# A two-layer graph network on one Trainium2 core: the first level of a top-p search from one ScalarE pass instead of two

## The chip, the cores and the metric

The kernel runs on one core of a Trainium2 chip. The core has TensorE (PE in the profile; PEld is its weight load), VectorE (DVE), ScalarE (ACT), GpSimd (POOL) and SyncE (SP, which issues DMAs). Each engine works through its own instructions in their order and waits at semaphores for the others.

The metric is the device time of one execution in microseconds. Before the change three executions took 1310.96, 1312.36 and 1307.9 us, with a median of 1310.96 us. The profile comes from a further execution that took 1361.88 us, of which the span from the first instruction to the last is 1360.1 us.

## The reference, cut to what matters

There are N = 2708 nodes with 256 features. Layer 0 multiplies a sparse adjacency matrix with the features. Layer 1 takes two steps; in each, every row of a softmax over all nodes is cut to its largest entries, which together hold 0.9 of the mass ("top-p"), and the cut rows multiply the features.

```python
def _top_p_attention(X, W1, W2, W3):
    q = X @ W1.T @ W2.T
    k = X @ W3.T
    logits = q @ k.T / TAU
    probs = jax.nn.softmax(logits, axis=-1)
    idx = jnp.argsort(-probs, axis=-1)
    sp = jnp.take_along_axis(probs, idx, axis=-1)
    cs = jnp.cumsum(sp, axis=-1)
    keep_sorted = cs - sp < TOP_P
    ...
    return A / jnp.maximum(A.sum(-1, keepdims=True), 1e-12)

for n in range(STEPS):
    A = _top_p_attention(Xa, W1, W2, W3)
    Xf = R @ Xf
    Xa = A @ Xa
    Z = Z + Xf @ U1[n].T + Xa @ U2[n].T
```

R is the row-normalised input to layer 1 (the adjacency with ones added on the diagonal). Two layer norms follow.

## The kernel before

The 2708 rows are cut into 22 blocks of 128 rows (the last, the "edge" block, has 20). A block's row of exponentials, 128 x 2708 numbers in float32, lies in SBUF as a tile `e`. In step 2 a row keeps too many entries for them to be sorted, so the cut is searched. Two trial levels `l0` and `l1` are tried; from what lies above each, the next is computed. A last level `l2` or `l1` is chosen; DVE then takes the largest 48 of what lies just below it and finds the cut among them exactly.

**Trying a level.** `try_act` (line 961) does it on ACT for blocks 1 to 21, `try_dve` (line 989) on DVE for block 0. With z the sum of a row's exponentials, an entry lies above the level when l*e > z. On ACT a try has two passes over the 2708 entries. Part 0 (line 966) is a Relu of l*e - z with its sum in `relu`; part 1 (line 969) is a Sign of the same with its sum in `sign`. Part 2 (line 972) turns the sum of signs into the count `n` of entries above the level; part 3 (line 974) makes `u` = relu/z + n, which is l times the mass above the level, and calls `next_level` (line 977): a line in l and u with the fitted constants `STEPS` (lines 979 and 980), and after the second try also `few` (line 982). On DVE one instruction (line 993) sums the entries above the level.

**The pipeline of step 2.** The loop at line 1272 runs 24 periods `per`, each of six slots `g`. In period `per` four blocks are under way at once:

- block per + 2 gets its logits from PE and its exponentials from ACT (`exps2`, lines 844 to 848, in slots 0, 1 and 3);
- block per + 1 has its levels tried on ACT;
- block per goes through `last_level` (lines 1003 to 1013), `below_level` (line 1023) and `candidates` (line 1030) on DVE; block per - 1 goes through `in_order`, `threshold`, `mark` (line 1083) and `mask` (line 1088) there;
- block per - 2 is turned on PE (`turn`, line 527), copied from PSUM to SBUF by ACT as `wT` (line 530) and multiplied on PE (`products`, line 564).

Beside these, PE works off the sparse product R with Xf in units of one 128 x 128 piece (`r_units`, line 749), three or so in a slot. Their right-hand sides `yg` are gathered by POOL's indirect DMAs (line 719). From period 12 on, rows that are done go through the layer norms, of which two to four 128 x 256 passes in slot 0 are ACT's (line 1192).

**What sets the order.** Nothing is scheduled automatically: the order of the calls in the loop is the order in each engine's queue. In one slot the calls are: turn, logits, r_units, products of the slot before, exps2, the parts of `try_act` for this slot, then DVE's share. In period `per` DVE first needs the end of the try of slot 3 of the period before: `last_level` reads `few`, `l1`, `u1`, `l2` and `relu`. In slot 5 of each period DVE runs `begin_search` (lines 852 to 857) of block per + 2, which needs the sum of the third exponential.

**Buffers that matter here.** `wT` and the PSUM tile `tr` have two buffers each, the PSUM tile `lg` of the logits has one, and `yg` has two.

**When the search fails.** Every row sets flags, such as one for more than 48 entries between level and cut. If any flag is set, the program runs `general_path`, which computes layer 1 again in a slow way. It is not run in the profile.

Of the kernel before, what the change touches and what calls it, by code (L numbers as in the profile page):

```python
# [11 lines left out]
AF = mybir.ActivationFunctionType  # L12
ALU = mybir.AluOpType
# [4 lines left out]
TOP_P = 0.9  # L18
# [12 lines left out]


GUESS = 2.76141059
STEPS = ((0.93339875, 14.44678062, 82.55022771), (0.98700001, 8.00991560, 128.06811957))
FEW = 20.0
TOP_S = 0.8999
TIE_EPS = 1.5e-5
KS = 7
# [110 lines left out]
def fast_path(ctx, tc, c, flags, fint, xT_d, x_d, w0_d, b0_d, w1_d, w2_d, w3_d, u1_d, u2_d, g_d, b_d):  # L149
    nc = tc.nc  # L150
    N, D, DA, NB, DC, KH, CHS, rows = c.N, c.D, c.DA, c.NB, c.DC, c.KH, c.CHS, c.rows
# [17 lines left out]
    def ps_acc(t=None):  # L169
        acc = ps.tile([P, CH], FP, tag="acc", name="acc")  # L170
        if t == NB - 1:
            nc.vector.memset(acc[:, :D + 1], 0.0)
        return acc
# [426 lines left out]
    def exps1(t):  # L600

        p = rows(t)
        e = es[t % 4]
        nmax, srt = st1[t]
        z = small.tile([P, 2], FP, tag="z1", name="z1", bufs=3)
        st1[t] = (srt, z)
        h = 11 * P

        def part(i):
            if i == 0:  # L610
                nc.scalar.activation(srt[:p], srt[:p], AF.Exp, bias=nmax[:p], scale=1.0)
            a, b = ((0, h), (h, N))[i]
            nc.scalar.activation(e[:p, a:b], e[:p, a:b], AF.Exp, bias=nmax[:p], scale=1.0,
                                 accum_out=z[:p, i:i + 1])
        return part
# [147 lines left out]
    def za_load(m):  # L763


        if loads.get(m):
            loads[m] = 2
            return None
        loads[m] = 1
        base = work.tile([P, D], FP, tag="in", name="base", bufs=3)  # L770
        nc.sync.dma_start(out=base[:rows(m)], in_=za_d[m * P:m * P + rows(m), :])
        return base
# [35 lines left out]
    def e2(t):  # L808
        return ring[t % 5]
# [30 lines left out]
    def shift(b, lg):  # L840
        nc.vector.tensor_reduce(b.nmax, lg[:, :P], AX.X, ALU.max, negate=True)
# [8 lines left out]
    def begin_search(b):  # L850

        nc.vector.tensor_reduce(b.z, b.all[:b.p, :NL], AX.X, ALU.add)
        yield
        nc.vector.reciprocal(b.rz, b.z)
        nc.vector.tensor_scalar(b.nz, b.z, -1.0, None, op0=ALU.mult)
        yield
        nc.vector.tensor_scalar(b.l0, b.roots, b.roots, b.rz, op0=ALU.mult, op1=ALU.mult)
# [21 lines left out]
    part = exps1(0)  # L879
# [5 lines left out]
    part = exps1(1)  # L885
# [11 lines left out]
    for t in range(NB):  # L897
        acc = ps_acc(t)
        part = exps1(t + 2) if t + 2 < NB else None
        b = None  # L900
        if t >= NB - 3:
            b = blocks[t - (NB - 3)] = Block(t - (NB - 3))
# [52 lines left out]
    w = tile1[:, NW:]  # L955
# [5 lines left out]
    def try_act(b, k, part):  # L961


        e = e2(b.t)[:b.p, :N]
        if part == 0:
            nc.scalar.activation(scr[:b.p, :N], e, AF.Relu, bias=b.nz, scale=b.l[k], accum_out=b.relu)  # L966
            return
        if part == 1:
            nc.scalar.activation(scr[:b.p, :N], e, AF.Sign, bias=b.nz, scale=b.l[k], accum_out=b.sign)  # L969
            return  # L970
        if part == 2:
            nc.scalar.activation(b.n, b.sign, AF.Identity, bias=halfn[:b.p], scale=0.5)
            return
        nc.scalar.activation(b.u[k], b.relu, AF.Identity, bias=b.n, scale=b.rz)
        next_level(b, k)

    def next_level(b, k):
        keep, slope, down = STEPS[k]
        nc.scalar.activation(b.kept, b.l[k], AF.Copy, scale=keep + TOP_P * slope, bias=-down)
        nc.scalar.activation((b.l1, b.l2)[k], b.u[k], AF.Identity, bias=b.kept, scale=-slope)  # L980
        if k:
            nc.scalar.activation(b.few, b.l1, AF.Copy, scale=TOP_P, bias=-FEW)

    def level(b, l):

        nc.vector.reciprocal(b.d, l)
        nc.vector.tensor_scalar(b.d, b.d, b.z, None, op0=ALU.mult)

    def try_dve(b, k):

        e = e2(b.t)[:b.p, :N]
        level(b, b.l[k])
        nc.vector.scalar_tensor_tensor(w[:b.p, :N], e, b.d, e, op0=ALU.is_ge, op1=ALU.mult, accum_out=b.m)
        nc.vector.tensor_scalar(b.u[k], b.m, b.rz, b.l[k], op0=ALU.mult, op1=ALU.mult)
        if k == 0:
            keep, slope, down = STEPS[0]
            nc.vector.tensor_scalar(b.kept, b.l0, keep + TOP_P * slope, -down, op0=ALU.mult, op1=ALU.add)
            nc.vector.scalar_tensor_tensor(b.l1, b.u0, -slope, b.kept, op0=ALU.mult, op1=ALU.add)

    def last_level(b):  # L1000
# [109 lines left out]
    def vector_slots(a, b, begin):  # L1110


        if b and b.t == 0:
            run_all(in_order(b))
            yield
            run_all(threshold(b))
            yield
            for i in range(WS):
                mark(b, i)
            yield  # L1120
            mask(b)
            yield
            run_all(last_level(a))
            below_level(a)
            yield
            run_all(candidates(a))
            run_all(begin)
            yield
            return
        order = in_order(b) if b else None  # L1130
        levels = last_level(a) if a else None
        cands = candidates(a) if a else None
        limits = threshold(b) if b else None
        run_all(turns((part_of_it(order, 7) if b else None, 1), (levels, 1)))
        yield
        if a:
            below_level(a)
        yield
        run_all(turns((order, 1), (part_of_it(cands, 8) if a else None, 2)))
        if a and not b:  # L1140
            run_all(part_of_it(cands, 8))
        yield
        run_all(turns((limits, 1), (cands, 2)))
        yield
        if b:
            mark(b, 0)
            mark(b, 1)
        yield
        for i in (2, 3):
            if b:  # L1150
                mark(b, i)
            if begin:
                next(begin)
        if begin:
            run_all(begin)
        if b:
            mask(b)
        yield
# [113 lines left out]
    for per in range(NB + 2):  # L1272
        if per == NB + 1:
            tail.append(True)
        n_r = units.get(per, 0)
        b_act = blocks.get(per + 1)
        t_mul = per - 2 if per > 1 else None
        if t_mul is not None:
            accs[t_mul] = ps_acc(t_mul)
        b_exp = None  # L1280
        if per and per + 2 < NB:
            b_exp = blocks[per + 2] = Block(per + 2)
        vector = vector_slots(blocks.get(per), blocks.get(per - 1), begin_search(b_exp) if b_exp else None)
        for g in range(NG):
            n = n_r * (g + 1) // NG - n_r * g // NG
            now = later.pop(0)
            later.append([])
            if g == 0:
                if b_exp:
                    shift(b_exp, lg[0])  # L1290
                r_units(n)
            if t_mul == EDGE:
                if g == 0:
                    products(0)
                    edge_product(ya, accs[EDGE], e2(EDGE))
            elif t_mul is not None:
                turn(t_mul, g, ya, accs[t_mul], e2(t_mul))
            if b_exp and g == 3:
                lg = logits(1, b_exp.t, 2)
            if g == NG - 1 and 3 < per + 3 < NB:  # L1300
                lg = logits(1, per + 3, 0)
            if g:
                r_units(n)
            if b_exp and g == 1:
                lg = logits(1, b_exp.t, 1)
            if t_mul is not None and t_mul != EDGE:
                products(1)
            if b_exp and g in (0, 1, 3):
                exps2(b_exp, (g + 1) // 2, *lg)
            if b_act:  # L1310
                for k, part in {0: ((0, 0),), 1: ((0, 1), (0, 2), (0, 3)), 2: ((1, 0),), 3: ((1, 1), (1, 2), (1, 3))}.get(g, ()):
                    try_act(b_act, k, part)
            next(vector)
            if g == 0:
                final_slot(0)
                if t_mul:
                    t = t_mul - 1
                    base = za_load(t)
                    later[0].append(lambda t=t, base=base: arrive(t, base, accs.pop(t), ras.pop(t)[:rows(t)]))
            for f in now:  # L1320
                f()
            if g and (per < NB + 1 or g < NG - 1):
                final_slot(g)
# [4 lines left out]
    for f in later[0] + later[1]:  # L1328
# [10 lines left out]
                                   op0=ALU.mult, op1=ALU.is_lt)  # L1339
# [391 lines left out]
```

## Time and profile before

| what | us |
|---|---|
| three executions, median | 1310.96 |
| profiled execution | 1361.88 |
| its span | 1360.1 |
| of the span: pipeline of step 2, first `below_level` to the last | 779.0 to 1300.6 |
| ACT: 43 Relu passes (line 966), all of step 2 | 113.6 |
| ACT: 42 Sign passes (line 969), all of step 2 | 110.9 |
| ACT idle in the 25.20 us period from 1126.36 | 2.90 |
| DVE idle in that period | 1.61 |
| PE idle in that period | 1.41 |

The table's idle times are a period's length less the busy time of the engine in it. A period is counted here from one `below_level` instruction on DVE to the next, which is a little after the start of slot 1. The groups of the page give the busy sum of a line and the mean duration of one instruction. The table of windows gives, for each stretch, every engine's busy time and the number of instructions. "Idle before" tells what an engine waited for; "issue" in that place means that no wait which the profile shows ended there. PE's ends are modelled, so its busy time holds some hidden waiting.

### The profile page before, as it was taken

To read this page: it belongs to the slowest core of one execution; us is meant where nothing else is said; L and a number is where in the kernel's file an instruction comes from. 1 tells how busy PE (TensorE), PEld (TensorE's weight loads), DVE (VectorE), ACT (ScalarE), POOL (GpSimd) and SP (SyncE) were. 2 spreads that over 40 slices of the span, in tenths; PEclk is the share of its full clock that TensorE was granted. 3 is DMA by queue.
4 is the path that set the end of the run, shared out by engine and by line. 5 is a ranking of instruction groups with operands and counts; after the bars stand their busy time and mean duration, and the time that the engine had idled before them with its cause. 6 is when DMAs were issued, how large, how long until landed. Compare 5 with 4: busy or idle time off the path is not lost.

```text
span 1360.1 us, 18883 instructions
## 1 busy us (share of the span) xinstructions
PE 1250.1 (92%) x5764; PEld 895.5 (66%) x5764; DVE 998.1 (73%) x3406; ACT 733.8 (54%) x1337; POOL 635.2 (47%) x594
## 2 busy tenths in 40 slices
PE   8999999988999999999997959999996999999985
PEld 6877877733567777666774727766664776666763
DVE  2544545866888888877840469878877899999995
ACT  1011011035455565555553577877786898998931
POOL 1000000014554533777563177777743668888850
PEclk9999999989899999999998969999998999999997
DMA  6554545513222110232222245645543444554541
GB/s 186 163 176 155 166 155 160 165 54 117 81 92 67 55 57 10 89 94 95 69 73 74 68 150 157 188 140 175 172 111 109 148 159 143 171 181 151 169 111 33
DMA packets 101993, 166.27 MB, mean 122 GB/s; under 512 B 17394, under 2 KB 74358, under 8 KB 101882
## 3 DMA queue, kind: packets, MB, share of 16 engines
q1 hardware_dynamic: 75596, 108.91, 24.7%
q0 software_dynamic: 20544, 51.17, 13.6%
q10 hardware_dynamic: 5742, 4.89, 1.3%
q8 instruction: 48, 0.79, 0.2%
q14 instruction: 63, 0.52, 0.1%
HBM read 130.87 MB, written 34.03 MB: 121 GB/s over the span
## 4 chain that ended last, share of the span: by engine, by line
PE 67%; ACT 19%; DVE 6%; issue 4%; another core or an unknown queue 2%; DMA 0%; ACTq 0%; DVEq 0%
PE acc L564 22%; PE acc L257 15%; PE lg L507 8%; PE tr L527 5%; PE misc L749 5%; ACT e L969 4%; ACT e L966 3%; ACT e L844 3%; ACT wT L530 3%; PE acc L651 2%; PE acc L462 2%; PE misc L426 2%; PE misc L392 2%; PE acc L672 2%
## 5 line engine op out<-in xcount | busy, mean ns | idle before, releaser
L530 ACT COPY wT<-tr 128x512 f32<-128x512 f32 (+2 forms) x258 | 131.7, 518 | 254.7 <-PE tr L527 153.3
L564 PE MATMUL acc<-ya,wT 128*128 128x256 f32 (+1 forms) x924 | 234.6, 394 | 18.8 <-ACT wT L530 12.1
L564 PE MATMUL acc<-x,wT 128*128 128x256 f32 (+1 forms) x924 | 234.6, 393 | 13.2 <-ACT wT L530 12.9
L719 POOL DMA_INDIRECT yg<-v_d,ix x154 | 190.1, 1234 | 79.4 <-issue 32.3
L564 PEld LDWEIGHTS acc<-x,wT 128*128 128x128 f32 (+1 forms) x924 | 167.2, 192 | 87.8 <-issue 40.6
L719 POOL DMA_INDIRECT yg<-yf_d,ix x154 | 192.6, 1250 | 62.3 <-issue 36.2
L564 PEld LDWEIGHTS acc<-ya,wT 128*128 128x128 f32 (+1 forms) x924 | 169.8, 193 | 75.6 <-issue 28.1
L257 PE MATMUL acc<-y,adj_t 128*128 128x257 f32 (+1 forms) x924 | 208.4, 381 | 0.0
L367 POOL DMA_INDIRECT adj_t<-in_adj,ix x154 | 170.3, 1106 | 51.4 <-issue 42.4
L749 PE MATMUL misc<-yg,adj_t 128*128 128x256 f32 (+1 forms) x704 | 183.5, 395 | 11.4 <-issue 6.6
L257 PEld LDWEIGHTS acc<-y,adj_t 128*128 128x128 f32 (+1 forms) x924 | 171.8, 189 | 32.7 <-issue 8.9
L507 PE MATMUL lg<-k,q 64*128 64x512 f32 (+3 forms) x528 | 151.9, 602 | 29.7 <-issue 11.2
L749 PEld LDWEIGHTS misc<-yg,adj_t 128*128 128x128 f32 (+1 forms) x704 | 125.7, 191 | 61.7 <-issue 31.2
L527 PE MATMUL tr<-ident,e 128*128 128x128 f32 (+2 forms) x946 | 147.0, 274 | 2.3 <-DVE e L1088 2.3
L527 PEld LDWEIGHTS tr<-ident,e 128*128 128x128 f32 (+2 forms) x946 | 113.6, 139 | 41.5 <-issue 17.6
L334 POOL DMA_DIRECT2D part_d<-e x1 | 0.6, 576 | 286.2 <-DVE e L333 286.2
L966 ACT ACTIVATE e<-e,st 128x2708 f32<-128x2708 f32 (+1 forms) x43 | 113.6, 2641 | 0.1
L570 DVE MAX8 cand<-e 128x8 f32<-128x170 f32 (+1 forms) x352 | 87.6, 318 | 32.7 <-ACT e L514 15.4
L969 ACT ACTIVATE e<-e,st 128x2708 f32<-128x2708 f32 (+1 forms) x42 | 110.9, 2641 | 0.1
L439 ACT COPY x1T<-tr 128x256 f32<-128x256 f32 (+1 forms) x22 | 8.0, 364 | 186.6 <-PE tr L438 186.6
L1030 DVE MAX8 cand<-w 128x8 f32<-128x136 f32 (+1 forms) x440 | 106.2, 285 | 0.0
L507 PEld LDWEIGHTS lg<-k,q 64*128 64x128 f32 (+1 forms) x528 | 39.3, 183 | 64.2 <-issue 35.6
(237 smaller groups left out, 1762.9 us busy)
## 6 DMA issues: line engine op xcount, KB each, us to landing
adj_t<-in_adj SPq DMA_DIRECT2D x44, 704.0 KB
adj_t<-adjc_d SPq DMA_DIRECT2D x44, 448.0 KB
adjc_d<-adj_t SPq DMA_DIRECT2D x22, 256.0 KB
base<-za_d SPq DMA_DIRECT2D x41, 128.0 KB
adjc_d<-adj_t SPq DMA_DIRECT2D x22, 192.0 KB
xt<-in_x ACTq DMA_DIRECT2D x21, 128.0 KB
x_d<-x SPq DMA_DIRECT2D x21, 128.0 KB
x1b_d<-xb SPq DMA_DIRECT2D x21, 128.0 KB
```

Of the source, the lines that this page charges most:

```text
L257: nc.tensor.matmul(acc[:p, :n], lhsT=halves[k // KH][:kw, k % KH, :p], rhs=y[:kw, k, :n], start=k == 0, stop=stop and k == NB - 1)
L367: nc.gpsimd.indirect_dma_start(out=a[:CW, i, :], out_offset=None, in_=adj_rows, in_offset=bass.IndirectOffsetOnAxis(ap=ix[:CW, m, i:i + 1] ...
L507: nc.tensor.matmul(lg[:p, h, :b - a], lhsT=q[o, t * P:t * P + p], rhs=keys[s][o, i, :b - a], start=True, stop=True)
L527: nc.tensor.transpose(tr[:kw, k % 4, :p], e[:p, k * P:k * P + kw], ident[:p, :p])
L530: nc.scalar.copy(wT[:, :full, :p], tr[:, :full, :p])
L564: nc.tensor.matmul(acc[:p, :D], lhsT=wT[:kw, k % 4, :p], rhs=y[:kw, k, :], start=k == 0, stop=k == NB - 1)
L570: nc.vector.max(dst[:p, i * 8:(i + 1) * 8], src[:p, i * step:i * step + w])
L719: nc.gpsimd.indirect_dma_start(out=y[:CW, i, :], out_offset=None, in_=rows_d, in_offset=bass.IndirectOffsetOnAxis(ap=ix[:CW, m, i:i + 1], ...
L749: nc.tensor.matmul(acc[:p, :D], lhsT=a[:kw, k, :p], rhs=y[:kw, k, :], start=k == 0, stop=k == CC)
L966: nc.scalar.activation(scr[:b.p, :N], e, AF.Relu, bias=b.nz, scale=b.l[k], accum_out=b.relu)
L969: nc.scalar.activation(scr[:b.p, :N], e, AF.Sign, bias=b.nz, scale=b.l[k], accum_out=b.sign)
L1030: nc.vector.max(b.cand[:p, 8 * i:8 * i + 8], low[:p, SEG2 * i:SEG2 * (i + 1)])
```

## The change

A first try on ACT has no Sign pass. The sum of the Relu pass, divided by z, goes straight into `u0`, and `next_level` follows from it. On DVE the first try sums max(e, d), with d = z/l the level itself, so that its sum has the same meaning plus N; the constant in line 997 takes the N out again. The second try stays as it was, in two passes. The fitted constants `STEPS` and `FEW` are others.

The slots change as well: the first try, now Relu pass and follow-up together, stands in slot 1; the Relu pass of the second try stands in slot 2 as before; its Sign pass with all that follows moves from slot 3 to slot 4.

```diff
-STEPS = ((0.93339875, 14.44678062, 82.55022771), (0.98700001, 8.00991560, 128.06811957))
-FEW = 20.0
+STEPS = ((0.63754, 5.05548, 149.26932), (0.91005, 11.45689, 138.22711))
+FEW = 34.21575
...
-        if part == 2:
+        if k == 0:
+            nc.scalar.activation(b.u0, b.relu, AF.Copy, scale=b.rz)
+        else:
             nc.scalar.activation(b.n, b.sign, AF.Identity, bias=halfn[:b.p], scale=0.5)
-            return
-        nc.scalar.activation(b.u[k], b.relu, AF.Identity, bias=b.n, scale=b.rz)
+            nc.scalar.activation(b.u1, b.relu, AF.Identity, bias=b.n, scale=b.rz)
         next_level(b, k)
...
-        nc.vector.scalar_tensor_tensor(w[:b.p, :N], e, b.d, e, op0=ALU.is_ge, op1=ALU.mult, accum_out=b.m)
+        if k == 0:
+            nc.vector.tensor_scalar(w[:b.p, :N], e, b.d, None, op0=ALU.max, op1=ALU.add, accum_out=b.m)
+        else:
+            nc.vector.scalar_tensor_tensor(w[:b.p, :N], e, b.d, e, op0=ALU.is_ge, op1=ALU.mult, accum_out=b.m)
...
-            nc.vector.tensor_scalar(b.kept, b.l0, keep + TOP_P * slope, -down, op0=ALU.mult, op1=ALU.add)
+            nc.vector.tensor_scalar(b.kept, b.l0, keep + TOP_P * slope, slope * N - down, op0=ALU.mult, op1=ALU.add)
...
-                for k, part in {0: ((0, 0),), 1: ((0, 1), (0, 2), (0, 3)), 2: ((1, 0),), 3: ((1, 1), (1, 2), (1, 3))}.get(g, ()):
+                for k, part in {1: ((0, 0), (0, 2)), 2: ((1, 0),), 4: ((1, 1), (1, 2))}.get(g, ()):
                     try_act(b_act, k, part)
```

## The prediction

> **What bounds the kernel now.** I read the busy shares first, then the chain of waits, then a table of windows that cuts step 2 into its periods, then the waits by engine in one stretch, and last ACT's timeline in one period.
>
> ```profile
> PE 1250.1 (92%) x5764; PEld 895.5 (66%) x5764; DVE 998.1 (73%) x3406; ACT 733.8 (54%) x1337; POOL 635.2 (47%) x594
> ...
> PE 67%; ACT 19%; DVE 6%; issue 4%; another core or an unknown queue 2%; DMA 0%; ACTq 0%; DVEq 0%
> ```
>
> Over the whole span PE leads, and ACT looks half idle. But the change is in step 2 alone, so the shares there decide (columns: window, its length, busy PE, PEld, DVE, ACT, POOL, then PE's clock and DMA):
>
> ```profile
> 892.92:920.43 27.51, 24.68 (x116) 17.77 (x115) 21.33 (x77) 20.03 (x33) 20.50 (x16) 1.00 0.53 163
> 1024.88:1053.47 28.59, 18.38 (x77) 12.57 (x75) 20.68 (x77) 20.14 (x33) 13.23 (x14) 0.83 0.39 120
> 1078.77:1102.12 23.35, 23.04 (x113) 17.21 (x111) 22.09 (x82) 20.32 (x35) 17.52 (x15) 1.00 0.54 170
> 1126.36:1151.56 25.20, 23.79 (x113) 16.97 (x112) 23.59 (x87) 22.30 (x39) 20.85 (x19) 1.00 0.55 167
> 1252.33:1277.26 24.93, 22.13 (x106) 16.09 (x105) 23.36 (x86) 22.25 (x39) 20.59 (x19) 1.00 0.53 163
> ```
>
> In the late periods three engines are within three microseconds of the period: PE 23.79, DVE 23.59, ACT 22.30 of 25.20. None is alone the bound; they wait for one another. The waits from 1126 to 1277 us, six such periods, say for what:
>
> ```profile
> PEld acc L564 <- ACT wT L530: 11.8, 15, 1.7
> DVE bulk L852 <- issue: 8.1, 6, 1.4
> PE acc L564 <- ACT wT L530: 5.5, 10, 1.3
> PE acc L564 <- ACT st L979: 2.6, 3, 0.9
> ```
>
> PE waits for ACT's copies wT; DVE has a single wait, 1.36 us in each period before L852, which reads the sum of the third exponential (ACT, L844). ACT's own order shows why both are late:
>
> ```profile
> 1129.79 2.63 ACT L966 ACTIVATE e<-e,st 128x2708 f32<-128x2708 f32 x1
> ...
> 1134.38 0.56 ACT L530 COPY wT<-tr 128x512 f32<-128x512 f32 x1
> 1134.85 1.11 ACT L844 ACTIVATE e<-lg,nmax 128x1024 f32<-128x1024 f32 x1
> ...
> 1135.95 2.64 ACT L969 ACTIVATE e<-e,st 128x2708 f32<-128x2708 f32 x1
> ...
> 1138.71 0.29 ACT L972 ACTIVATE st<-st,halfn 128x1 f32<-128x1 f32 x1
> 1139.04 0.39 ACT L974 ACTIVATE st<-st 128x1 f32<-128x1 f32 x1
> 1139.33 0.19 ACT L979 ACTIVATE st<-st 128x1 f32<-128x1 f32 x1
> ...
> 1139.75 0.56 ACT L530 COPY wT<-tr 128x512 f32<-128x512 f32 x1
> ...
> 1143.32 0.82 ACT L844 ACTIVATE e<-lg,nmax 128x660 f32<-128x660 f32 x1
> ```
>
> The copy of slot 2 at 1139.75 stands behind the Sign pass L969 and its followers, and so does the third exponential at 1143.32. ACT is full from slot 0 to slot 3 and free for 2.6 us only at the period's end.
>
> **What the skill says.** The Trainium skill, "ScalarE: Activation LUTs", section "What ACT_TABLE_LOAD costs", prices an ACTIVATE at 186 ns plus 0.833 ns an element plus about 93 ns for each [128,1] pointer operand. A pass over 2708 entries with two pointers is then 2628 ns; the trace has 2641, so they agree. "Perfetto Trace Analysis", section "Optimizing Scalar/DVE Operations", says that Scalar or Vector can cause bubbles on other engines without being saturated; the waits above are such. Its section "Identifying the Most-Contended Engine" warns that matmul busy time misleads; here PE's 23.79 against 23.04 for like work at 1078 shows it, 0.75 us of "busy" being hidden waiting.
>
> **Part 1: the Sign pass goes.** From the start of L969 at 1135.95 to that of L979 at 1139.33 are 3.38 us. In its place comes one small Copy with one pointer operand. The nearest rows are L979 (0.19, none) and L980 (0.29, one); I take 0.29. ACT loses 3.1 us for each of 21 blocks, 65 us in all. What that is worth on the path differs by stage.
>
> *Late periods (1102 to 1300).* DVE's stream is unchanged, so its busy time is the floor. Of its idle time I leave 0.2 us a period. The windows 1102 to 1277 have idle 0.98, five times 1.6, and 1.57: 10.55 less 7 x 0.2 = 9.1. The last, 1277 to 1300, has 0.38 and gives 0.2. PE can follow: its period without waits was 23.35 at 1078. The window 1078 has PE idle of 0.31 only and gives nothing. Sum 9.3.
>
> *Early periods (822 to 1025).* DVE has 4 to 6 us to spare; PE's waits count. L564 waits 1.3 for wT and 1.0 with no releaser shown. Matmul starts further apart than their usual step beside L564 add, by my count of gaps, 1.5 more hidden in "busy". The 1.9 of L507 for L848 stay, since slot 0's exponentials don't move; so do 5.6 us of L749, which waits for gathered yg. Sum 3.8; I take 3.5, because faster PE waits longer for the gathers.
>
> *The window 1024 to 1053.* No sparse units run in period 10, and PE waits for ACT 4.3 us at L564 and more at L507. One Sign pass less is worth up to 3.1 in the first slots, and as much again where the last copies no longer stand behind a Sign pass in slot 3. But ACT itself waits 4.6 us there for PE. I take 3, bounds 0 and 6.
>
> *The start (774 to 822).* Period 0 is a run of passes on ACT, and 3.1 us go. PE's next logits then still wait behind L749, whose gathers land at 788 and 790. Period 1 has a 6 us wait on ACT that has nothing to do with passes. I take 2, bounds 0 and 5.5.
>
> **Part 2: the slots.** The first Relu pass moves from slot 0 to slot 1, the second Sign pass from slot 3 to slot 4. Slot 0 of a late period has two exponentials and four norm passes (L1192) on ACT; without the Relu pass the slot 1 copy comes 2.7 us earlier. Behind the Sign pass in slot 4 stand the copies of slot 5 and the roots of the norms; PE needs the slot 5 copy only in the next period's slot 0. The copy of slot 4, for which PE waits today behind Sign and five followers, gets in front. These effects are in the sums above.
>
> The move adds one wait that counts: DVE's L1003 at the next period's start needs L982. Before, L982 ends at 1148.12 and L1003 starts at 1149.14: 1.0 us to spare. After, ACT reaches slot 4 at about 1141.8 in the same period; the turn of slot 4 on PE starts at 1142.20 today and about 1 us earlier without PE's waits. From a copy at 1141.9: 0.5 copy, 2.8 Sign with its read, 1.3 followers, so 1146.5. DVE's start moves up 1.4, to 1147.7. Still 1.2 to spare, so I cost it at nothing; if the cover goes, each microsecond is a microsecond of the period, since all of `last_level`, L1023 and the candidates are queued behind L1003.
>
> **Part 3: DVE's first try** happens once. L993 took 3.04 us. No such instruction is in the trace over 2708 entries: between 1.5 (if it ran at two entries a cycle) and 3.1 us. DVE then waits 6.3 us for ACT (L1003 at 777.84), and ACT starts its pass at 774.55, after PE's last projections. Worth nothing at either end. The constants change no instruction.
>
> **Sum.** 9.3 + 3.5 + 3 + 2 = 17.8, so 18 us off 1361.88: 1343.9. The profiled execution stands 3.9% over the median shown; I scale by 1310.96/1361.88 = 0.9626 and get 1293.6 us.
>
> **Rivals.**
> - *Only DVE's floor moves (late periods).* The early stretch is then held by gathers: POOL busy 20.50 of 27.51, its 0.3 us steps between gathers apart. 9.3 us: 1352.6, scaled 1302.
> - *More goes.* A wait-free early period would take 24.2 us (23.35 at 1078 and two more sparse units at 0.43 each, 1.30 us for three on PE's timeline). The six windows from 866.75 to 1024.88 last 158.1, so 13 are to be had; with 5 at period 10, 3 at the start and 11 late: 32 us, scaled 1280. For it: the chain from 893 to 917 is ACT nearly throughout. Against: PE was idle there only 2.83 us, two of them for gathers.
> - *Slower: the Sign pass in slot 4 comes too late for L1003.* Once (911.37) ACT's copy waited 3.7 us for PE after its transposes had been issued. If the copy of slot 4 meets that in every period, L1003 comes 3.7 - 1.2 = 2.5 us late. In the seven late periods DVE has no slack: 17.5 us lost against 9.3, and the early gain is gone in the same wait: 8 us slower, scaled 1319. It beats the gains from about 1.3 us of lateness a late period on.
> - *The change doesn't do what it says:* a level from the sum alone may be worse, a row has over 48 entries below it, a flag is set and `general_path` runs. It has 27 DVE passes for each of 22 blocks in two steps; at 3.04 us each 3612 us, so near 4900. The profile can't tell.
> - *Nothing moves:* 1311, if every wait is replaced at once.
>
> **How the numbers follow.** Chances: forecast 0.50, late only 0.20, more 0.13, nothing 0.05, slot 4 late 0.09, general path 0.03. A measurement of this kernel can't tell less than 0.3%, 4 us, from no change. Faster 0.83, same 0.05, slower 0.12. The range from 1279 to 1307 holds the first three; the cases outside are under 2 in 10.
>
> **What would show it.** 21 instructions on L969 instead of 42. Late periods of about 23.8 us with DVE idle under 0.4 and no wait before L852. No PE wait for wT at L564. L1003 without a wait. Wrong if late periods stay over 25, if L1003 waits for L982 in most periods, or if the early periods stay at 27 with longer L749 waits (then the gathers hold them).

## The result and the profile after

The changed kernel takes 6509.67 us (six executions, 6506.45 to 6511.52), the kernel before 1309.43 us beside it: 4.969 times as long, with an interval of 4.959 to 4.979. The forecast was 1293.6 us. What happened is the prediction's rival "The change doesn't do what it says", to which it gave 3 chances in 100.

The first lines of the page, the chain of work that ended last and the costliest groups of the kernel after (a group's columns: line, engine, operation, tiles, number; busy time and mean ns; idle time ahead of it and who ended most of it):

```profile
PE 2858.0 (44%) x11676; PEld 1985.5 (31%) x11676; DVE 5949.8 (91%) x8774; ACT 1288.1 (20%) x2235; POOL 753.8 (12%) x682
...
PE   9999999871243044214304322322431431432331
...
DVE  4698689859999999999999989999999999999998
...
DVE 77%; PE 19%; issue 2%; ACT 2%; POOL 0%; DMA 0%; SPq 0%; DVEq 0%; ACTq 0%; POOLq 0%
...
L1520 DVE SCALAR_TENSOR_TENSOR scr<-e,cand 128x2708 f32<-128x2708 f32 (+1 forms) x1188 | 3630.0, 3056 | 49.7 <-ACT e L1499 4.1
...
L1543 DVE TENSOR_TENSOR_SCAN scr<-scr,before 128x1354 f32<-128x1354 f32 (+1 forms) x88 | 267.3, 3038 | 3.1
```

Each digit of the two rows stands for a fortieth of the span, 163 us. In the first eight PE is at work as before; from the tenth on DVE is the only full engine. Line 1520 isn't in the profile of before: it is the bisection of `general_path`, 27 passes for each of 22 blocks in two steps, 1188 in all. The windows say when it begins (columns: window, length, then busy time and number of instructions of PE, PEld, DVE, ACT and POOL, PE's clock, DMA share, GB/s):

```profile
0.00:1237.00 1237.00, 1192.06 (x5538) 866.06 (x5538) 952.65 (x3263) 662.92 (x1241) 620.86 (x581) 0.98 0.44 132
1283.00:6504.00 5221.00, 1624.12 (x5914) 1090.50 (x5914) 4957.79 (x5386) 614.15 (x968) 119.47 (x88) 0.62 0.05 16
```

The last `below_level` begins at 1236.9 us and the number of flags is cast to an integer at 1282.9 us. Up to there the program does what it was meant to do, at about the pace of before. Then at least one flag is set, and layer 1 is computed once more in 5221 us.

### The profile page after: what moved, and what is told of

Same layout as the page of the kernel before. It is cut to its first block, busy times and chain, and to the rows that moved or that the text cites. A ratio compares the mean times of both kernels' runs of the same rounds, so it can differ in the third digit from the quotient of the medians.

```text
span 6504.7 us, 37928 instructions
## 1 busy us (share of the span) xinstructions
PE 2858.0 (44%) x11676; PEld 1985.5 (31%) x11676; DVE 5949.8 (91%) x8774; ACT 1288.1 (20%) x2235; POOL 753.8 (12%) x682
## 4 chain that ended last, share of the span: by engine, by line
DVE 77%; PE 19%; issue 2%; ACT 2%; POOL 0%; DMA 0%; SPq 0%; DVEq 0%; ACTq 0%; POOLq 0%
DVE scr L1520 56%; PE acc L564 6%; DVE scr L1543 4%; PE acc L257 3%; PE lg L507 2%; DVE e L1548 2%; DVE scr L1546 2%; DVE scr L1536 2%; DVE nmax L1490 2%; PE misc L749 2%; DVE cand L1522 2%; DVE th L1523 1%; PE tr L527 1%; DVE cand L1516 1%; DVE scr L1542 1%
## 5 line engine op out<-in xcount | busy, mean ns | idle before, releaser
L1520 DVE SCALAR_TENSOR_TENSOR scr<-e,cand 128x2708 f32<-128x2708 f32 (+1 forms) x1188 | 3630.0, 3056 | 49.7 <-ACT e L1499 4.1
L1573 PE MATMUL tr<-ident,e 128*128 128x128 f32 (+1 forms) x968 | 178.1, 314 | 3031.1 <-DVE e L1548 2992.7
L1421 PE MATMUL acc<-v,adj_t 128*128 128x256 f32 (+1 forms) x968 | 264.9, 440 | 435.1 <-DMA adj_t<-in_adj 431.8
L1421 PEld LDWEIGHTS acc<-v,adj_t 128*128 128x128 f32 (+1 forms) x968 | 207.9, 219 | 491.2 <-issue 450.1
L1482 PE MATMUL lg<-qk 64*128 64x512 f32 (+1 forms) x528 | 318.4, 766 | 61.3 <-ACT e L1484 61.3
L1564 PE MATMUL acc<-ya,wT 128*128 128x256 f32 (+1 forms) x968 | 278.3, 438 | 2.7 <-ACT wT L1576 2.6
L1543 DVE TENSOR_TENSOR_SCAN scr<-scr,before 128x1354 f32<-128x1354 f32 (+1 forms) x88 | 267.3, 3038 | 3.1
L1564 PE MATMUL acc<-x,wT 128*128 128x256 f32 (+1 forms) x968 | 253.8, 408 | 2.6 <-ACT wT L1576 2.6
L564 PE MATMUL acc<-ya,wT 128*128 128x256 f32 (+1 forms) x924 | 230.7, 389 | 0.4 <-ACT wT L530 0.4
L564 PE MATMUL acc<-x,wT 128*128 128x256 f32 (+1 forms) x924 | 230.5, 388 | 0.0
L1421 PE MATMUL acc<-yf,adj_t 128*128 128x256 f32 (+1 forms) x968 | 222.9, 389 | 0.0
L1421 PEld LDWEIGHTS acc<-yf,adj_t 128*128 128x128 f32 (+1 forms) x968 | 179.8, 189 | 41.4 <-issue 13.6
```

The costliest lines, as they stand in the source:

```text
L564: nc.tensor.matmul(acc[:p, :D], lhsT=wT[:kw, k % 4, :p], rhs=y[:kw, k, :], start=k == 0, stop=k == NB - 1)
L1421: nc.tensor.matmul(acc[:p, :n], lhsT=halves[k // KH][:kw, k % KH, :p], rhs=y[:kw, k, :n], start=k == 0, stop=stop and k == NB - 1)
L1482: nc.tensor.matmul(lg[:p, :b - a], lhsT=qk[o, 0, t * P:t * P + p], rhs=qk[o, 1, a:b], start=True, stop=True)
L1520: nc.vector.scalar_tensor_tensor(scr[:p, 0, :], e[:p], cand[:p, j:j + 1], e[:p], op0=ALU.is_ge, op1=ALU.mult, accum_out=mass[:p, j:j + 1])
L1543: nc.vector.tensor_tensor_scan(run, eq, eq, before[:p], op0=ALU.add, op1=ALU.bypass)
L1564: nc.tensor.matmul(acc[:p, :D], lhsT=wT[:kw, k - k0, :p], rhs=y[:kw, k, :], start=k == 0, stop=k == NB - 1)
```

## Experiments

Two questions. Why was a flag set? And what is the change worth where none is? The letters below stand for these theories.

- **A:** one row (or a few) of step 2 needs more than 48 entries below its last level. The rival: the fast path fails in many rows, or in another test.
- **F:** the profile on which the prediction rests was not like the executions that give the time, so that some of its waits were not there to be removed.
- **G:** GpSimd's queue, gathers and norm products, holds the late periods. The rival is the prediction's sum: they fall to DVE's floor and the time falls with them.
- **H:** the rival of the prediction, the Sign pass in slot 4 too late for line 1007 (line 1003 before).

### One flag, one row

A model of step 2 in plain arithmetic on the reference's inputs gives, for each row, the number of entries between last level and cut. With the constants of before the largest number is 48. With the new ones and one pass less, one row has 51, row 74 of block 20: the level `l1` that follows from its first try is 1819.2 where before it was 1955.7, its last level 2110.2 where before it was 2181.1, and it had 43 entries between. All others stay at 48 or below. The first experiment clears the flag of this test for 32 rows of that block alone, so it leaves out one test of 32 rows:

```diff
+    nc.vector.memset(flags[64:96, 4 * NB + 20:4 * NB + 21], 0.0)
     nc.vector.tensor_reduce(fcol, flags, AX.X, ALU.add)
```

> The changed kernel, but the flags that tell a lost cut (the fifth group, 4*NB to 5*NB) of rows 64 to 95 of block 20 are set to zero before all flags are counted; a row flagged there keeps the fast path's result. Theory A: the new constants leave one row alone, row 74 of block 20, with 51 entries between its last level and its cut where 48 are listed, and its one flag sends the whole layer the slow way. Then the slow way isn't taken and the time is that of the fast path, 1265 to 1285 us. Rival B: a level from the sum alone is too coarse for many rows in many blocks: the slow way is taken, 6500 us. Rival C: the flag comes from another group (cut above the level, or ties): 6500 us.

Measured: 1301.84 us, ratio to before 0.993 (0.9907 to 0.9952). The slow way is gone, so every flag that was set lies in these 32 rows of one block, and in this test. The time is 17 us above the upper end of what had been expected of it; that is the second question.

The second experiment leaves the flags alone and raises one constant by 6%, which in the model brings this row from 51 to 46 and leaves 48 as the largest number of all:

```diff
-STEPS = ((0.63754, 5.05548, 149.26932), (0.91005, 11.45689, 138.22711))
+STEPS = ((0.63754, 5.05548, 149.26932), (0.91005, 12.14430, 138.22711))
```

> The changed kernel with one constant moved by 6 per cent: the slope of the second step 12.1443 instead of 11.45689. No instruction differs. Theory A: the row with 51 entries gets its level nearer to the cut, no flag is set, 1265 to 1285 us. Rival B (the one pass cannot place the levels of many rows): 6500 us. If the time is 6500 here and fast in the run without that flag, the row is right and the sum worked out for it on paper is not.

Measured: 1299.84 us, ratio 0.9918 (0.9897 to 0.994): no slow way, with the same instructions and the same limit. The third keeps the changed constants and takes more entries (`TOP2 = 56` for `TOP2 = 48`):

> The changed kernel with its own constants, but with the exact part of the search taking the largest 56 entries below the level instead of 48. Theory A (the one row needs 51): no flag, so no slow way; each block pays for one more round of eight on DVE, 0.5 to 1 us, on 22 blocks: 1303-1320. If the flag came from another test than this limit, the time stays near 6500.

Measured: 1376.72 us on a chip where the kernel before takes 1366.46, ratio 1.0077 (1.0047 to 1.0107). No slow way here either: three ways to take the flag away, and A stands. The runs narrow it to 32 rows of one block; that it is row 74 alone is the model's word. The chip is a matter of its own, see below.

For the rest the constants were fitted anew to the one-pass rule (`STEPS = ((0.6293539, 4.47718, 179.69807), (0.98026414, 12.085015, 99.442345))`, `FEW = 26.728706`; largest number of entries 43 in the model). This "refit kernel" is the change as it was meant.

> The changed kernel with all seven constants fitted anew, so that by arithmetic on the inputs no row needs more than 43 entries below its last level (limit 48) and no cut lies above it. No instruction differs from the changed kernel. Theory A: no flag, 1265 to 1285 us, about 30 us under before: ratio 0.97 to 0.98. Rival B: 6500 us. By the prediction's own sum for the fast path 1293.6; by the trace of the changed kernel's fast path, whose step 2 pipeline is 39 us shorter than before's, 1270.

Measured: 1301.95 us, ratio 0.9932 (0.9911 to 0.9952). So with no flag set the change is worth 8 us, not 18.

### Which profile to count on

The kernel before was profiled once more, beside others:

> The kernel before, unchanged, profiled a second time. Its first profile took 1361.88 us, 51 us over the median of its other executions; the kernel with refitted constants was profiled at 1304.5 us and gained only 8 us by the median. Theory F (the first profile of before was an execution of its own, slower in and outside step 2, so that its waits overstate what can be gained): the second profile spans 1305 to 1315 us, first below_level at about 755 us instead of 779, windows of early periods near 24.5 us instead of 26.9, and few waits of PE for wT or for gathers. Rival G (profiling slows this kernel whenever ACT is fuller): again about 1360 us.

Measured: 1306.15 us with its profile, span 1304.3 us. Its windows, cut at the same `below_level` instructions as those of the refit kernel under it (start, early periods, period 10, three periods, late periods, rest):

```profile
754.34:808.37 54.03, 42.22 (x172) 29.20 (x171) 53.05 (x191) 48.98 (x76) 43.37 (x36) 0.91 0.58 177
808.37:978.24 169.87, 167.63 (x798) 123.52 (x798) 148.08 (x536) 139.51 (x231) 128.48 (x103) 1.00 0.57 168
978.24:1001.52 23.28, 18.75 (x84) 13.24 (x83) 20.56 (x77) 19.93 (x33) 14.09 (x13) 0.93 0.41 133
1001.52:1072.40 70.88, 69.56 (x332) 51.42 (x331) 65.97 (x242) 61.58 (x105) 50.91 (x44) 1.00 0.50 158
1072.40:1223.34 150.94, 141.02 (x656) 100.78 (x655) 141.34 (x512) 133.76 (x234) 124.81 (x109) 1.00 0.54 167
1223.34:1304.30 80.96, 61.46 (x333) 46.08 (x331) 68.02 (x226) 31.25 (x64) 31.01 (x29) 0.88 0.32 87
```

The late periods are those of the first profile, 25.20 us each. The early ones are not: the six windows that took 158.1 us there are 23.8 to 24.5 each here, 145.3 in all, and PE is busy in 167.63 of the 169.87 us of the second row. PE was already full, and there was nothing for ACT's spare time to give. Period 10 took 28.59 us there and 23.28 here, the first window 32.70 there and 22.91 by the same count here. F holds for the start and the early periods: their terms, 2 and 3.5 of the sum's 17.8 us, were counted for the most part on waits that the usual execution doesn't have. In the second row PE waits only for ACT's line 848, 2.2 us in all, and not once for `wT`. In period 10 the wait that the prediction counted on is there, only smaller: PE waits 2.9 us for `wT`, where the first profile has 4.3.

The refit kernel was run a second time, beside three others on one chip (before there: 1310.15 us):

> The refit kernel once more, beside the three others of this call on one chip. On a chip where the kernel before takes about 1309 us: 1300-1304, ratio 0.993, as in its first run. On a chip where the kernel before takes about 1365 us (as in the first profile of all): theory H (ACT's slot 4 is too late for line 1007 as soon as PE is late by 2 us in it, the rival of the prediction) expects 1370-1380, slower than before by 0.3 to 1%; the prediction's sum expects 1347, ratio 0.987.

Measured: 1300.01 us, ratio 0.992 (0.9899 to 0.9941). Its windows:

```profile
759.17:813.20 54.03, 42.67 (x174) 29.71 (x173) 53.05 (x191) 40.17 (x67) 43.37 (x36) 0.87 0.59 178
813.20:981.33 168.13, 166.31 (x793) 122.70 (x792) 149.09 (x535) 120.01 (x210) 126.19 (x103) 1.00 0.59 170
981.33:1003.64 22.31, 20.75 (x94) 14.18 (x93) 20.57 (x77) 18.23 (x32) 13.43 (x12) 0.92 0.43 133
1003.64:1070.83 67.19, 66.41 (x319) 49.91 (x319) 65.81 (x242) 52.01 (x95) 54.48 (x46) 1.00 0.54 169
1070.83:1216.72 145.89, 140.98 (x670) 104.05 (x668) 142.03 (x511) 116.89 (x217) 121.46 (x105) 0.99 0.55 170
1216.72:1302.20 85.48, 63.87 (x325) 46.91 (x324) 68.06 (x226) 28.00 (x60) 34.02 (x32) 0.84 0.33 87
```

Row by row the gain is 0, 1.7, 1.0, 3.7, 5.1 and then minus 4.5 us: what the late periods give is handed back after them. (These are two single executions; the first row starts 4.8 us later in the second, and in the other kernels with the change anywhere from 754.3 to 758.7.)

Of the 3.7 us of the fourth row 2.6 fall in its first period. Period 10 and this one together took 46.6 us before and take 43.0 here, and PE's wait for `wT` is gone. On the chips of 1309 us every other kernel without the pass in these two periods takes 41.3 to 43.3 us for them, with new slots or old; the one that has both passes in the new slots takes 46.1. In these two periods the gain belongs to the missing pass; how much of it lasts to the end is the next question.

### What holds the late periods

The groups of POOL in the late stretch, first the second profile of before, then the refit kernel:

```profile
L719 POOL DMA_INDIRECT yg<-v_d,ix x85 | 108.7, 1279 | 25.0 <-issue 13.0 <-PE tr L527 3.7 <-PE misc L749 3.0
L1207 POOL TENSOR_TENSOR yg<-yg,gb 128x256 f32<-128x256 f32 x12 | 8.8, 730 | 0.5
L1208 POOL TENSOR_TENSOR yg<-yg,x1b 128x256 f32<-128x256 f32 x12 | 8.7, 728 | 0.9
```

```profile
L719 POOL DMA_INDIRECT yg<-v_d,ix x81 | 105.2, 1298 | 23.7 <-issue 12.2 <-PE misc L749 4.3 <-PE tr L527 3.0
L1211 POOL TENSOR_TENSOR yg<-yg,gb 128x256 f32<-128x256 f32 x12 | 9.0, 746 | 0.1
L1212 POOL TENSOR_TENSOR yg<-yg,x1b 128x256 f32<-128x256 f32 x12 | 8.8, 731 | 0.9
```

The idle time of the gathers is 25.0 us for 85 of them, 0.29 each, and 23.7 for 81: POOL's waits in both stretches, listed by releaser, have a longest of 0.3 us without exception. That is the step between one gather and the next, not waiting. Adding busy time and steps, 108.7 + 25.0 + 8.8 + 8.7 gives 151.2 of 150.94 us before, and 105.2 + 23.7 + 9.0 + 8.8 gives 146.7 of 145.89 after. (The sums are a little over the stretch because an instruction at its edge is counted whole.) POOL is full in the late stretch of both kernels.

In the refit kernel it is full for much longer. From its first gather of `v_d` (the second half of the 308 gathers), at 986.9 us, to the end of the last of 154, at 1252.8, POOL has no wait over 0.3 us: these 265.9 us are its own work and its steps, and the span ends 49.4 us later. In the second profile of before the same stretch takes 271.7 us, with four longer waits of 9.0 us in all. The longest is for the norm pass that ACT does in slot 0:

```profile
POOL yg L1207 <- ACT yg L1192: 6.4, 1, 6.4
```

POOL's stretch is 5.8 us shorter in the refit kernel, and from period 10 to the end it takes 320.9 us instead of 326.1. A period that ends sooner only leaves more gathers for the end. That POOL's waits make the difference was read from two traces and not tried.

Most gathers take 0.95 us, some over three. POOL and DVE of the refit kernel at the same moment (start, duration, line, and in brackets the idle time ahead):

```profile
1165.99 0.95 POOL L719 DMA_INDIRECT yg<-v_d,ix  x1 [0.30 <-PE acc L564]
1167.24 3.21 POOL L719 DMA_INDIRECT yg<-v_d,ix  x1 [0.30 <-PE tr L527]
1170.75 0.95 POOL L719 DMA_INDIRECT yg<-v_d,ix  x1 [0.31 <-issue]
```

```profile
1166.58 3.05 DVE L1027 SCALAR_TENSOR_TENSOR w<-e,st 128x2720 f32<-128x2720 f32 x1
```

The gather ends 0.82 us after the pass. Of the 265 gathers from 800 us on, 36 take over 2 us; each of them starts while a full-width pass of DVE is under way and ends 0.81 to 0.83 us after it. The 31 that were under way when such a pass began take their usual 0.95 us. The Trainium skill, "SBUF — State Buffer", section "SBUF: two separate sides", warns of this: a gather issued by GpSimd has its descriptors made by GpSimd's own cores, and DVE can hold the port pair that they share for the length of an instruction. The page tells it of a DMA beside a copy on DVE. The trace agrees for the passes here, as far as times can show it: a gather that starts during the pass takes 2.7 to 3.6 us, 1.7 to 2.7 more than usual.

Does it matter that POOL is full? The next kernel leaves out POOL's two norm products. It was measured twice, first on the chip of 1366 us:

```diff
             h = self.h
-            nc.gpsimd.tensor_tensor(h[:p], h[:p], c.gb[:p, 0, :], op=ALU.mult)
-            nc.gpsimd.tensor_tensor(h[:p], h[:p], self.x1[:p], op=ALU.add)
```

> The refit kernel without POOL's two norm products (lines 1211 and 1212): the output lacks the first norm's gain and the addition of the residual. If POOL is full in the last periods, its load falls by these two products (about 2 us a period) and every period from 1060 us on stands at DVE's floor, 23.7-24.0, as the prediction's sum had it: 1294-1298 in all. If something else holds 25.2 there (ACT's third exponential, PE), the periods stay near 25 and the time stays within 2 us of the refit kernel's 1302.

Measured there: 1350.34 us, ratio 0.9867 (0.9836 to 0.9899).

> The refit kernel without POOL's two norm products (lines 1211 and 1212): the output lacks the first norm's gain and the addition of the residual. On a chip of 1309 us: if these products behind the gathers hold the last periods at 25.2, all late periods are 23.5-24.0 and the time is 1293-1298; if not, within 2 us of the refit kernel. On a chip of 1365 us: 1350, as in its first run.

Measured beside the refit kernel: 1287.41 us, ratio 0.9825 (0.9801 to 0.9849), 12.6 us below the refit kernel and well below the 1293 to 1298 expected. Its late stretch and the rest, two of its late periods and, for comparison, one of the refit kernel from the end of the stretch:

```profile
1068.20:1207.62 139.42, 137.88 (x667) 103.78 (x666) 137.93 (x512) 116.29 (x216) 105.27 (x85) 1.00 0.58 182
1207.62:1285.40 77.78, 60.99 (x330) 45.32 (x328) 65.83 (x226) 28.23 (x61) 18.81 (x16) 0.88 0.29 86
1091.56:1114.83 23.27, 23.01 (x112) 17.22 (x111) 23.03 (x87) 19.40 (x36) 16.01 (x15) 1.00 0.59 182
1161.30:1184.57 23.27, 23.01 (x112) 17.13 (x112) 23.03 (x87) 19.40 (x36) 17.82 (x15) 1.00 0.58 181
```

```profile
1166.58:1191.75 25.17, 24.20 (x117) 17.64 (x116) 23.73 (x87) 20.21 (x40) 20.89 (x19) 1.00 0.55 167
```

With the products gone every late period is 23.0 to 23.4 us to the end, with PE and DVE within 0.26 us of full in the two shown; and from the last but one `below_level` to the end of the span it takes 77.8 us where the refit kernel takes 85.5. POOL now has waits of up to 2.1 us among its gathers. G holds: leaving out the products is worth 12.6 us.

Why it is more than expected shows in DVE. In the six late periods DVE waits 2.4 us less, since the product of line 1212 that its statistics waited for is gone, and its busy time falls by 4.1 us (142.03 to 137.93) for as many instructions: together the 6.5 us by which the stretch is shorter. Some of DVE's small instructions take longer in the kernel with products, above all this one, first in the refit kernel, then without them (min/median/max in ns):

```profile
L1082 DVE TENSOR_SCALAR part<-part,st x6: 241/734/758, 1082.3 to 1202.6; 128x32 f32<-128x32 f32 x6
L1082 DVE TENSOR_SCALAR part<-part,st x6: 240/241/243, 1079.0 to 1195.4; 128x32 f32<-128x32 f32 x6
```

So the products cost more than their time in POOL's queue: DVE's busy time, on which the prediction built its floor, depends on where they fall. How much of the 12.6 us is the queue and how much DVE isn't told apart by this run.

Could the wait alone be moved? DVE's statistics (line 1186) wait for the norm product in slot 3, 3.6 us in the last periods. One slot later:

```diff
-        if i == 3:
+        if i == 4:
             for k, f in enumerate(new + finals):
                 f.stats(k)
```

> The refit kernel, with the norm statistics (bn_stats of the rows that POOL's line 1212 has just finished) in slot 4 instead of slot 3. Theory G (GpSimd's queue holds the last periods: DVE stands in slot 3 behind a norm product that stands behind gathers): the wait of the statistics for line 1212 shrinks from 3.6 us in six instances to under 1, the last four full periods fall from 25.2-24.7 to 23.7-24.3, and the time goes from 1302 to 1296-1299. Rival (POOL is simply full there, 20.9 us busy and 4.3 of steps between gathers in 25.2): the wait only changes its place, the periods stay near 25 and the time stays 1300-1303. The prediction's sum (every late period at DVE's floor) would give 1296-1298.

Measured on the chip of 1366 us: 1377.76 us, ratio 1.0054 (1.0031 to 1.0077).

> The refit kernel with the norm statistics in slot 4. On a chip of 1309 us: theory G (GpSimd's queue holds DVE there) expects 1296-1299 and late periods of 23.7-24.3; the rival (POOL is full, the wait only changes its place) 1300-1304. On a chip of 1365 us: 1375-1380 as in its first run, so that nothing new is learned on theory G.

Measured: 1299.34 us, ratio 0.9909 (0.9886 to 0.9932); beside it the refit kernel had 1300.01. The time lies between the two forecasts. The last two of the six late periods do fall, to 23.9 and 24.1 us, as the first expected, but the rest of the span grows from 85.5 to 86.6 us. PE's waits from 1040 to 1245 us, of this kernel and then of the refit kernel:

```profile
PE misc L749 <- DMA yg<-v_d,ix: 9.2, 13, 2.7
```

```profile
PE misc L749 <- DMA yg<-v_d,ix: 1.2, 2, 0.8
```

The wait for GpSimd's products has in large part become PE's wait for GpSimd's gathers, and the total is the same. That is what a full engine looks like: a wait for it can be moved, not removed.

### Which pass is worth something

Two kernels give the refit kernel one unused Sign pass back in slot 1, in the early periods or in the late ones:

```diff
-{1: ((0, 0), (0, 2)), 2: ((1, 0),), 4: ((1, 1), (1, 2))}
+{1: ((0, 0), (0, 1), (0, 2)) if per < 10 else ((0, 0), (0, 2)), 2: ((1, 0),), 4: ((1, 1), (1, 2))}
```

> The refitted kernel with the first try's Sign pass put back in slot 1 in periods 0 to 9 alone; its sum is used by nothing. 10 passes of 2.76 us, 27.6 us of ACT. If the early periods hold most of the gain (PE waits there for ACT): 1304 to 1308. If they are held by PE's own work with ACT free: 1302, no change.

Measured: 1305.1 us, ratio 0.9962 (0.9943 to 0.998). With `per > 11` in place of `per < 10`:

> The refitted kernel with the first try's Sign pass put back in slot 1 in periods 12 to 20 alone; its sum is used by nothing. 9 passes, 25 us of ACT. By the prediction's sum the late periods are worth 9 us of the gain: 1308 to 1311. If GpSimd's queue of gathers and norm products holds the late periods at 25.2 us with or without the pass: 1302 to 1305.

Measured: 1299.36 us, ratio 0.9925 (0.9906 to 0.9944). One extra pass of 2.64 us in nearly every late period costs nothing in the total. It isn't free on the way: DVE waits for the third exponential again, 6.4 us in the six late periods. But the products fall elsewhere: the wait for line 1212 is gone and DVE's busy time is 138.63 us instead of 142.03, so that the six periods take 146.45 us, where the refit kernel takes 145.89 and the kernel before 150.94; and the rest takes 80.4 us instead of 85.5. POOL is full from the first gather of `v_d` to the last here too. So the missing pass of the late periods, to which the prediction gave half its sum, 9.3 us, is worth nothing in the total.

The kernel with the pass in the early half is 3 to 5 us slower than the refit kernel (1305.1 against 1301.95 and 1300.01, on other chips; the intervals of the first pair overlap). Its trace says where: the first three periods take 58.25 us instead of 54.03, and the early periods behind them 169.20, where two profiles of the refit kernel have 169.25 and 168.13. With the old slots both passes fit into 54.03 us there. So this loss is one of the pass's place in slot 1 at the start, and no gain of the early periods from the missing pass is shown by it.

### The slots

The kernel before with the new slots and both passes of the first try:

```diff
-{0: ((0, 0),), 1: ((0, 1), (0, 2), (0, 3)), 2: ((1, 0),), 3: ((1, 1), (1, 2), (1, 3))}
+{1: ((0, 0), (0, 1), (0, 2), (0, 3)), 2: ((1, 0),), 4: ((1, 1), (1, 2), (1, 3))}
```

> The kernel before, two passes and old constants, with the new slots alone: the whole first try (Relu and Sign) in slot 1, the second Relu in slot 2, the second Sign with all that follows in slot 4. Theory A (the gain of the fast path comes from the 2.8 us of ACT work that goes, the slots only spread it): about 0 to -10 us against before, 1300 to 1310. Rival D (the slots are what helps, since the copy of slot 4 gets in front of a Sign pass): -20 us or more, 1285. Rival E (the Sign pass in slot 4 comes too late for last_level): slower than before, and a wait at L1003 for L982 in most periods.

Measured: 1313.78 us, ratio 1.0029 (1.0018 to 1.0039), a little slower than before. It isn't E: line 1003 waits for line 982 only twice. Most of the loss stands in the first three periods again, 58.93 us instead of 54.03. And the refit kernel with the old slots, `{0: ((0, 0),), 1: ((0, 2),), 2: ((1, 0),), 3: ((1, 1), (1, 2))}`, twice:

> The changed kernel with refitted constants, but the passes at their old places: first Relu in slot 0, its follow-up in slot 1, second Relu in slot 2, second Sign with all that follows in slot 3. Theory A (the missing pass is the gain, slots matter little): within 2 us of the refitted kernel with new slots, 1300 to 1304 us. Rival D (slots and pass help only together): 1306 to 1310, as before.

Measured: 1303.95 us, ratio 0.9962 (0.9946 to 0.9979).

> The refit kernel with the passes in the old slots (first pass in slot 0, Sign pass in slot 3). On a chip of 1309 us: 1303-1306, as in its first run. On a chip of 1365 us: theory H expects that the wait of line 1007 for the end of the try is gone and that the time falls below that of the refit kernel and of the kernel before, 1352-1363; if the slots have nothing to do with it, it is as slow as the refit kernel, within 4 us.

Measured: 1303.82 us, ratio 0.995 (0.9931 to 0.9968), where the refit kernel beside it has 0.992 (0.9899 to 0.9941). So the missing pass alone, with the old slots, is worth 5 to 6 us against before, and that is clear of the noise. The intervals of old and new slots overlap, so that the new slots help the one-pass kernel by some 3 to 4 us more is likely rather than shown. It fits that with the old slots POOL still has one wait for ACT's norm pass, 2.9 us, and with the new ones none.

### The chip of 1366 us

On one chip the kernel before takes 1366.46 us (28 executions from 1363.51), about as long as in the first profile. There both kernels with the changed search and all of their work are slower than before: the one with 56 entries, which has one more round on DVE in each block, and the one with the later statistics. The refit kernel itself wasn't measured there. DVE's waits from 1104 to 1300 us of the kernel with the later statistics, and those of the kernel before from 1053 to 1278 us in the first profile:

```profile
DVE st L1007 <- ACT st L983: 14.9, 5, 3.7
DVE st L1007 <- issue: 3.1, 1, 3.1
```

```profile
DVE bulk L852 <- issue: 8.9, 7, 1.4
DVE bulk L852 <- ACT e L844: 4.9, 2, 3.9
```

This is the wait of H in the trace: line 1007 waits for the end of the try in slot 4, up to 3.7 us at a time, 15.8 us in six waits from 1028 us on; on the other chips the refit kernel has no such wait in its late periods. On the same chip the kernel with 56 entries has 7.0 us of it from 1104 us on, and the kernel without the norm products a single one of 3.0 us. That the slots are the cause of the loss on that chip wasn't tried by putting them back there, and stays open.

## Why the prediction was wrong

**The failed step** is that the sum took the fast path for granted: it put `general_path` at nothing, and the rival "The change doesn't do what it says" at 0.03, with the remark that the profile can't tell. The runs show one row's flag and 5221 us of `general_path` in its place. The profile can't tell, but the inputs can. The number of entries under the last level is settled by the inputs and the constants, and no trace is needed to work it out. The limit of 48 was met exactly by one row of the kernel before, so new constants for a coarser first level had no room; another row, which had 43, came to 51, and one row of 2708 brought 5200 us. It was the constants and not the missing pass as such: with other constants the same instructions set no flag. The rival's size was off too. Its one term, 3612 us for line 1520, measured 3630.0. It left out everything else in `general_path`, 5221 less 3630, or 1591 us: scans (267.3 for line 1543), the logits, the products, the copies. "Near 4900" was 6510.

What the sum says without the flag, term by term, against the windows of the two kernels:

- *ACT loses 65 us:* ACT's busy time fell from 735.4 to 675.7, and 63 instructions are gone, three a block. That is 59.7 us of busy time, where the 65 counted the steps between instructions too. The cost of the edit was about right; what it was worth wasn't.
- *Late periods, 9.3:* the six that hold 8.4 of it gave 5.1 us, and 4.5 came back after them. The floor was put at DVE's busy time. Four to five periods do reach it, at 23.4 to 24.2, as forecast; in the last two DVE waits 1.2 us each for POOL's product. The prediction showed POOL's 20.85 busy of 25.20 and set its 0.3 us steps apart only for the early periods. For the late ones the same addition on the same profile says that POOL was full: four norm products and fourteen to fifteen gathers a period, with 4.35 us of "idle" that is all steps. A full queue isn't shortened by what DVE and ACT save.
- *Early periods 3.5, start 2:* 1.7 and 0. Where "L749 waits for gathered yg" stays and PE waits for ACT were read from an execution 51 us over the median. The scale factor 0.9626 spread that difference evenly; it was in particular waits.
- *Period 10, 3:* 1.0 us in it and 2.6 in the next, 3.6 together. This term had the wait, the cause and the size right. The next period, the window 1053 to 1078, stands in no term of the sum.
- *No wait at line 1003, 1.2 us to spare:* held in the late periods where the kernel before takes 1309 us. On the other chip, in the kernel with the later statistics, the wait comes at 2.6 us on average (15.8 us in six), near the rival's 2.5, and with the sign that it gave.
- *DVE's first try:* worth nothing, as said: the new instruction takes 3.03 us, the old one 3.04, and the start is 54.03 us in both.

The real gain of the change as meant is 8 to 10 us, 0.7 to 0.8%, less than the forecast's 17.4. With other constants the change is faster, as forecast, but that does little for the sum: the total is about half of it, and its largest term is worth nothing. The refit kernel beats both kernels on the usual chips. So do those of 1299.84, 1299.36 and 1299.34 us, and none of them is to be told from it.

## What to carry to other kernels

Where a kernel has a guarded fast path, the first question on a change of its numbers is how far the worst row is from the guard, and that is a question for the inputs; a guard met exactly has no room. Before a wait on one engine is priced, add up busy time and fixed steps between instructions of every engine in that stretch: POOL at 83% busy was full. Don't take an engine's busy time for a fixed floor either: DVE's fell from 142.0 to 137.9 us in six periods when another engine's work went. And take a second profile of the kernel before when the first stands 4% over its times: a difference like that sits in particular waits.

## What was not expected of the hardware

Two kinds of chip, or of condition, for one kernel: 1309.1 to 1310.2 us in four comparisons and 1366.5 us in one. In the profiles with the longer time the landings of most gathers have no record (the view of DMAs gives 3.6 and 3.3 us to landing for the second profile of before, and no figure for the first):

```profile
yg<-yf_d,ix POOLq DMA_INDIRECT x154
yg<-v_d,ix POOLq DMA_INDIRECT x154
```

```profile
yg<-yf_d,ix POOLq DMA_INDIRECT x154, 3.6
yg<-v_d,ix POOLq DMA_INDIRECT x154, 3.3
```

The packets of GpSimd's queue took as long in both (a median of 159 ns in the early periods of each), yet in the first PE and POOL both stood still once in most early periods, PE for 1.0 to 1.7 us and POOL for 2.0 to 2.5, and PE's wait has no releaser on record. Why isn't known; it stays open.
